# Dealing side work out to TensorE by its time beside a selective scan, taking its results up later, and summing more softmax rows on ScalarE

## The chip, the core and the metric

The kernel runs on one core of a Trainium2 chip, in float32. The metric is the device time in microseconds (us) of one execution, from start to end. Lower is better.

## The reference, cut to what matters

Four layers work on `x` of shape (4, 128, 64, 64), that is four images of 128 channels and 4096 pixels. The change touches the first three.

```
# layer 0: for every image
u  = groupnorm(x)
s  = scores(u)        # depthwise 3x3, gelu, channel attention, depthwise 3x3, gelu, head, variance
order = argsort(-patch_mean(s))            # 256 patches of 4x4 pixels
x1 = layernorm(u[order] + pe[order])
xc = silu(conv1d(x1 @ in_proj));  z = x1 @ in_proj_z
dt = softplus(...);  B, C = xc @ x_proj
h_t = exp(dt_t * A) * h_(t-1) + dt_t * B_t * xc_t     # 256 channels x 16 states, 4096 steps of t
y   = (sum over states of h * C + D * xc) * silu(z)
x   = x + (y @ out_proj)[inverse order]
# layer 1
x   = x + conv3x3(groupnorm(x), 128 -> 128 channels) + bias
# layer 2, attention part: for every image, 16 heads of 8 numbers, 4096 tokens
q   = ring(ln(t)) per head;  e = exp(q q^T / sqrt(8))   # symmetric
ctx = (e @ q) / rowsum(e);   then a projection, norms and a small feed-forward part
# layer 2, second part, and layer 3: expert layers and a linear attention (not touched)
```

## The kernel before

**Layers 0 and 1** are in `layers01`. The image's pixels stand along the free dimension, in eight chunks of 512. Three sections follow each other: the first image is brought into scan order alone (`in_order(0)`), then one long scan section treats all four images, then the last image is finished alone (`end(3)`).

The scan section has 32 chunks (four images of eight), and each chunk has eight steps `g`, one for two of the 16 states. A step does this:

- TensorE spreads two rows of B over the partitions into the PSUM tile `b_ps`, of which there is one buffer.
- VectorE multiplies `dtx` by `b_ps` into `hs` (L637), and then runs four scans of 128 x 512 (L641). Each scan takes its factors from a PSUM tile `decay`, which ScalarE makes with an Exp (L640). There are two such tiles.
- GpSimd copies the carry (L644) and multiplies `hs` by C (L647, two instructions), with C broadcast from DRAM by the DMAs `c_sb<-c_d`.
- TensorE sums over the states into `y_ps`, one step later (`add`).

Between these steps the program places three other kinds of work.

- `enter(n + 1)` makes the inputs of the next chunk: products `xc_ps`, `z_ps`, `dbc_ps`, `dt_ps`, activations Silu (L541, L519), Exp and Ln, three GpSimd products, and DMAs that double the results into `dt2` and `dtx2`. It is a generator whose steps are taken one in a scan step.
- `leave(n)` finishes the chunk before: two VectorE instructions (L592), a GpSimd product with the gate `sz` (L595), the product `out_ps`, and a ScalarE copy (L600).
- `others(b)` is what this text calls the work beside the scan. It is `end(b - 1)`, which puts the image before back into its pixel order and convolves it (`put_back`, then `convolve` with `groupnorm_padded` and `conv3x3`), followed by `in_order(b + 1)`, which prepares the next image.

The work beside is a generator too. It stops at 141 points where both parts exist, at 106 for the first image, and at 35 for the last. The count of stops decides how much is placed in a scan step:

```python
due = BESIDE * (NG * c + g) // (NG * NCH - NG - 1) if c > 0 or g > 1 else 0
```

`BESIDE` is 140, so two or three stops fall on a step, whatever lies between them: a 3x3 convolution of a whole chunk (9 products of 512 columns) counts as one stop, as a tiny group norm product does. A stop's products and the instruction that takes up their result from PSUM stand together in the program. All of these products draw on the same three PSUM buffers (tag `mm`).

In the scan section the order of TensorE's instructions is the order in which the program writes them (`manual_schedule(engines={PE})`). The order on VectorE, ScalarE, GpSimd and the DMA queue is made by a scheduler that starts from the program's order.

Exp and Tanh use one function table of ScalarE; Gelu, Silu, Ln and Sqrt use others, and a change of table is an instruction of its own (ACT_TABLE_LOAD).

**Layer 2's attention** goes image by image, head by head. For a head, 16 pairs of key tiles `m` meet four blocks of 1024 queries `j`. Because `e` is symmetric, only pairs with `m // 4 >= j` are computed. A step (one `j`, one `m`) has four score products, two Exps of 128 x 1024 on ScalarE (L1153), and eight passes of `ctx_ps`. In a step with `m // 4 > j` (the program calls it `behind`) VectorE also transposes both Exps in 32 x 32 blocks into `turned` (L1140, L1159), for later products `acc_ps`, and the row sums of the Exps are needed. The row sums come in one of two ways. Either ScalarE's accumulator delivers them, at one ACTIVATION_READ_ACCUMULATOR after each Exp; or GpSimd folds the step's two Exps twice (L1101, L1102), and VectorE reduces the quarter, five steps later (L1146). The function `folded` chooses. TensorE, VectorE and GpSimd keep the program's order here.

A step of the `behind` kind needs, on VectorE, two transposes. The order of steps inside a block is three, two or one `behind` steps and then one on the diagonal.

Of the kernel before, what the change touches and what calls it, by code (L numbers as in the profile page):

```python
# [9 lines left out]
F32 = mybir.dt.float32  # L10
# [19 lines left out]
class Common:  # L30
# [3 lines left out]
    def __init__(self, tc, pool):  # L34
        nc = self.nc = tc.nc
# [85 lines left out]

    def groupnorm_padded(self, xb, xp, small, psum):
# [4 lines left out]
        for c in range(NCH):  # L127
            nc.vector.bn_stats(st[:, c, :], xb[:, c * CH : (c + 1) * CH])
            if c % 2:
                yield  # L130
        mv = small.tile([P, 2], F32, name="gn_mv")
        nc.vector.bn_aggr(mv, st)
        yield
        mp = psum.tile([P, 1], F32, name="gn_mp", tag="mm")
        self.mm(mp, self.group_mean, mv[:, 0:1])
        gm = small.tile([P, 1], F32, name="gn_gm")
        nc.vector.tensor_copy(gm, mp)
        d = small.tile([P, 1], F32, name="gn_d")
        nc.vector.tensor_tensor(d, mv[:, 0:1], gm, ALU.subtract)
        v2 = small.tile([P, 1], F32, name="gn_v2")  # L140
        nc.vector.scalar_tensor_tensor(v2, d, d, mv[:, 1:2], ALU.mult, ALU.add)
        yield
        vp = psum.tile([P, 1], F32, name="gn_vp", tag="mm")
        self.mm(vp, self.group_mean, v2)
        sd = small.tile([P, 1], F32, name="gn_sd")
        nc.scalar.activation(sd, vp, AF.Sqrt, bias=self.eps5)
        rs = small.tile([P, 1], F32, name="gn_rs")
        nc.vector.reciprocal(rs, sd)
# [3 lines left out]
        nc.gpsimd.memset(xp[:, 1 : HW + 1, HW + 1 : HW + 2], 0.0)  # L152
        off = small.tile([P, 1], F32, name="gn_off")
        nc.vector.scalar_tensor_tensor(off, gm, -1.0, rs, ALU.mult, ALU.mult)
        yield
        for c in range(NCH):
# [7 lines left out]
            if c % 2:  # L164
                yield

    def conv3x3(self, ps, taps, xp, c):

        for k in range(9):
# [4 lines left out]
                xp[:, 8 * c + ky : 8 * c + ky + 8, kx : kx + HW],  # L174
# [43 lines left out]
def layers01(K, xd, dpool, w, w1):  # L218
# [6 lines left out]
    BESIDE = 140  # L225
    with ExitStack() as ctx:
# [81 lines left out]

        deep1 = depthwise(w["conv1_w"], "deep1")
# [6 lines left out]
        def in_order(b, made, work, psum):  # L316
# [39 lines left out]
            yield  # L356
            unders = [under, gather(xp, 1)]
            for c in range(NCH):
                ps = convolved(unders.pop(0), deep1)
                nc.scalar.activation(  # L360
# [8 lines left out]
                yield  # L369
# [4 lines left out]
            yield  # L374
# [3 lines left out]
            nc.scalar.activation(c1, c1p, AF.Relu)  # L378
            yield
# [3 lines left out]
            nc.scalar.activation(ca, c2p, AF.Sigmoid)  # L383
# [4 lines left out]
            for c in range(NCH):  # L388
# [5 lines left out]
                nc.scalar.activation(sq, mp, AF.Square)  # L394
                yield
                ps = convolved(unders.pop(0), deep2)
                f2 = work.tile([P, CH], F32, name="f2", tag="ln_xc")
                nc.scalar.activation(f2, ps, AF.Gelu, bias=conv2_b, scale=ca)
                if c + 2 < NCH:
                    unders.append(gather(fp, c + 2))  # L400
                yield
# [3 lines left out]
                nc.scalar.activation(pv, vp, AF.Tanh, scale=5.0)  # L405
                yield
# [3 lines left out]
                nc.scalar.activation(sc, hp, AF.Tanh, bias=head_b, scale=0.5)  # L410
                yield
# [7 lines left out]
                yield  # L419
# [4 lines left out]
            for h in range(2):  # L424
# [12 lines left out]
                yield  # L437
# [6 lines left out]
            for h in range(2):  # L444
# [10 lines left out]
                yield  # L455
# [4 lines left out]
            for c in range(NCH):  # L460
# [11 lines left out]
                yield from K.layernorm_steps(xl, x1, work, psum)  # L472
                yield
# [8 lines left out]
                yield  # L482
# [5 lines left out]
            for o in range(0, 16, 2):  # L488
# [5 lines left out]
                nc.vector.tensor_copy(ts, tp)  # L494
                yield
# [3 lines left out]
                nc.scalar.copy(by_rank[:, o : o + 2, :], pp)  # L499
                yield  # L500
            made.append((xq, perm_inv))

        def scan(seqs, others, work, psum, psbc, psex, psy):
# [17 lines left out]
            def enter(n):  # L521
# [9 lines left out]
                for d in range(2):  # L531
# [10 lines left out]
                    if n > 0:  # L542
                        gate(n - 1, d)
# [43 lines left out]
            def leave(n):  # L587
# [8 lines left out]
                yield  # L596
                op = psum.tile([P, CH], F32, name="out_ps", tag="mm")
                for d in range(2):
                    mm(op, out_projT[:, d, :], xc[:, d, :], start=d == 0, stop=d == 1)
                nc.scalar.copy(seqs[b][0][:, c * CH : (c + 1) * CH], op)  # L600
# [26 lines left out]
            for n, (b, c) in enumerate(chunks):  # L627
                if c == 0:
                    carry = small.tile([P, NG, NQ], F32, name="carry", bufs=2)
                    nc.vector.memset(carry, 0.0)  # L630
                    beside, done = others(b), 0
# [1076 lines left out]
```

## Time and profile before

| what | us |
|---|---|
| median of three runs | 11060.14 (11053.74 to 11065.5) |
| the profiled execution, its own time | 11065.94 |
| its span in the trace | 11064.2 |
| first image alone, up to the first decay | 273.6 |
| scan section, first decay to last | 2842.9 |
| of it, images 0, 1, 2, 3 | 695.2, 761.6, 760.9, 625.3 |
| the last image's end and the first image's attention inputs | 288.7 |
| the four attention blocks | 1370.4, 1375.6, 1373.6, 1375.4 |
| between them, three times | 270 to 271.3 |
| everything after | 1352.0 |

An image's share of the scan section runs from its first `decay` to the next image's first. An attention block runs from its first score product to its last. In the views of waits a row reads: engine, tile and line of the instruction that was late, then what released it, then the sum, the number and the longest of such waits. In the view of stretches a row gives the stretch, its length, and then for each engine the busy time and the number of instructions, at last the granted TensorE clock, the DMA share and the rate.

### The profile page before, as it was taken

How to read it: one execution, taken by the hardware profiler on the slowest of the kernel's cores; microseconds unless marked ns; L12 is line 12 of the kernel's file. 1: busy time of each engine (PE TensorE's matmuls, PEld its weight loads, DVE VectorE, ACT ScalarE, POOL GpSimd, SP SyncE). 2: the span in 40 equal slices, each digit the busy share in tenths (PEclk: the TensorE clock that was granted, in tenths of full speed). 3: DMA queues.
4: the chain of work that ended last, by engine and by line, in shares of the span. 5: the costliest groups of instructions: out<-in, count | busy, mean ns of one | idle time of the engine just before them, and what ended most of it. 6: DMA issues, size and time to landing. Idle time of an engine off the chain costs nothing. (4 is left out here: it accounts for less than half of the span.)

```text
span 11064.2 us, 183405 instructions
## 1 busy us (share of the span) xinstructions
PE 9097.1 (82%) x71376; PEld 3379.2 (31%) x71376; DVE 7816.5 (71%) x8718; ACT 7349.4 (66%) x9690; POOL 6134.3 (55%) x3623
## 2 busy tenths in 40 slices
PE   5777878778766999968999968999968999966767
PEld 2222223223122333323333323333323333323433
DVE  2688687687846887867788867888757788744563
ACT  2565464654526999857998857989958889932431
POOL 0466455455626777736777736777737777720000
PEclk8787888878778999979999979999979999977888
DMA  3322322322212121222221121212122112122004
GB/s 86 82 71 52 97 60 57 100 63 64 54 48 42 33 37 35 33 72 36 36 36 33 32 77 34 38 32 33 32 77 38 33 33 33 32 87 87 22 16 137
DMA packets 524325, 581.54 MB, mean 53 GB/s; under 512 B 106232, under 2 KB 329536, under 8 KB 520896
## 3 DMA queue, kind: packets, MB, share of 16 engines
q1 hardware_dynamic: 523456, 569.81, 22.2%
q8 instruction: 563, 9.22, 0.4%
q14 instruction: 306, 2.51, 0.1%
HBM read 373.96 MB, written 76.55 MB: 41 GB/s over the span
## 5 line engine op out<-in xcount | busy, mean ns | idle before, releaser
L1153 ACT ACTIVATE ex<-score 128x1024 f32<-128x1024 f32 x5120 | 4904.9, 1031 | 555.5 <-issue 221.2
L1101 POOL TENSOR_TENSOR folded<-ex 128x1024 f32<-128x1024 f32 x960 | 2293.0, 2389 | 1163.5 <-ACT ex L1153 1131.4
L89 PE MATMUL ctx_ps<-ex,qt 128*32 128x512 f32 x20480 | 2723.7, 596 | 0.0
L1159 DVE STREAM_TRANSPOSE turned<-ex 128x1024 f32<-128x1024 f32 x1536 | 1892.0, 1232 | 479.2 <-ACT ex L1153 394.2
L89 PE MATMUL acc_ps<-turned,turned_v 128*32 128x256 f32 x24576 | 1827.5, 389 | 220.2 <-DVE turned L1140 218.8
L1140 DVE STREAM_TRANSPOSE turned<-ex 128x1024 f32<-128x1024 f32 x1536 | 1854.7, 1207 | 0.0
L89 PE MATMUL score<-queries,keys 32*128 32x512 f32 x10240 | 1358.8, 497 | 124.5 <-ACT ex L1153 74.7
L641 DVE TENSOR_TENSOR_SCAN hs<-decay,carry,hs 128x512 f32<-128x512 f32 x1024 | 1248.2, 1263 | 153.4 <-ACT decay L640 144.1
L640 ACT ACTIVATE decay<-dt,a_neg 128x512 f32<-128x512 f32 x1024 | 699.9, 690 | 876.7 <-DVE hs L641 873.1
L1102 POOL TENSOR_TENSOR quarters<-folded 128x512 f32<-128x512 f32 x960 | 1234.5, 1286 | 75.3
L647 POOL TENSOR_TENSOR hs<-hs,c_sb 128x1024 f32<-128x1024 f32 x512 | 1202.2, 2370 | 47.8 <-DMA c_sb<-c_d 28.0
L89 PEld LDWEIGHTS score<-queries,keys 32*128 32x128 f32 x10240 | 523.5, 182 | 2183.5 <-issue 1670.8
L89 PEld LDWEIGHTS acc_ps<-turned,turned_v 128*32 128x32 f32 x24576 | 561.7, 108 | 937.6 <-issue 543.9
L89 PE MATMUL y_ps<-hs,pair 128*64 128x512 f32 x2048 | 657.3, 760 | 225.1 <-POOL hs L647 225.1
L89 PEld LDWEIGHTS ctx_ps<-ex,qt 128*32 128x32 f32 x20480 | 684.7, 110 | 463.3 <-DVE ctx L1083 53.4
L637 DVE TENSOR_TENSOR hs<-dtx,b_ps 128x2048 f32<-128x2048 f32 x256 | 581.6, 2272 | 321.2 <-PE b_ps L89 227.2
L644 POOL COPY carry<-hs 128x4 f32<-128x4 f32 x256 | 65.2, 255 | 1110.3 <-DVE hs L641 1095.8
L1146 DVE TENSOR_REDUCE dacc<-quarters 128x2 f32<-128x512 f32 x960 | 617.4, 648 | 0.0
L1083 DVE COPY ctx<-ctx_ps 128x512 f32<-128x512 f32 x256 | 177.2, 692 | 564.2 <-PE ctx_ps L89 564.1
L89 PE MATMUL ln_var<-ln_sq,mean 128*128 128x512 f32 x448 | 297.1, 750 | 223.6 <-ACT ln_sq L104 188.2
L973 POOL TENSOR_TENSOR turned_v<-v,quarter 128x1024 f32<-128x1024 f32 x192 | 459.0, 2392 | 16.7 <-DMA v<-value_d 11.1
L89 PE MATMUL b_ps<-dbc,spread 32*128 32x512 f32 x512 | 341.7, 751 | 145.8 <-DVE hs L637 145.8
(344 smaller groups left out, 9306.9 us busy)
## 6 DMA issues: line engine op xcount, KB each, us to landing
c_sb<-c_d SPq DMA_DIRECT2D x512, 128.0 KB
queries<-head_d SPq DMA_DIRECT2D x1024, 64.0 KB
keys<-head_d SPq DMA_DIRECT2D x1024, 64.0 KB
dt<-dt SPq DMA_DIRECT2D x128, 256.0 KB
dtx<-dtx SPq DMA_DIRECT2D x128, 256.0 KB
w<-in_L_ffn_weight SPq DMA_DIRECT2D x32, 1024.0 KB
w<-in_L_ffn_weight SPq DMA_DIRECT2D x128, 256.0 KB
under<-xp SPq DMA_DIRECT2D x384, 66.0 KB
```

Source lines behind the costliest of these rows:

```text
L89: self.nc.tensor.matmul(out, lhsT, rhs, start=start, stop=stop)
L637: nc.vector.tensor_tensor(hs, dtx2, bb.unsqueeze(1).to_broadcast([P, NQ, CH]), ALU.mult)
L640: nc.scalar.activation(ex, dt2[:, q, :], AF.Exp, scale=a_neg[:, q, g : g + 1])
L641: nc.vector.tensor_tensor_scan(hs[:, q, :], ex, hs[:, q, :], carry[:, g, q : q + 1], ALU.mult, ALU.add)
L647: nc.gpsimd.tensor_tensor(at, at, cs.unsqueeze(1).to_broadcast([P, 2, CH]), ALU.mult)
L973: nc.gpsimd.tensor_tensor(t, v.unsqueeze(2).to_broadcast([P, 4 * BT, 4, HD]), quarter.unsqueeze(1).to_broadcast([P, 4 * BT, 4, HD]), ALU.mult,
L1101: nc.gpsimd.tensor_tensor(hs, exs[:, :, 0], exs[:, :, 1], ALU.add)
L1102: nc.gpsimd.tensor_tensor(qs, hs[:, :, 0 : CH // 2], hs[:, :, CH // 2 :], ALU.add)
L1140: nc.vector.transpose(*upright)
L1146: nc.vector.tensor_reduce(at, qs, AX.X, ALU.add)
L1153: nc.scalar.activation(ex, sps[p], AF.Exp, scale=scale, accum_out=dacc[:, j, h, t : t + 1] if summed else None)
L1159: nc.vector.transpose(*upright)
```

## The change

The change has six parts.

1. The stops of the work beside the scan carry a cost each, in units near a microsecond of TensorE, and the scan deals out by sums of costs (`COST_END` 127.2 for `end`, `COST_ORDER` 215.2 for `in_order`). The total is that of the parts which the image has, so the first and the last image's work is spread over seven chunks as well. Inside a chunk the table `ROOM` gives 4% of the chunk's share up to the second step, 21% up to the fourth, and then 20% to each of the last four.
2. Instructions that take up a product's result are not written with it, but put on a list (`K.late`), which is emptied (`flush`) at fixed places of a scan step, ahead of the next piece of work beside.
3. The entry of a chunk begins at step 0, not 1, and has one step more: the second half of `xc_ps` and both `z_ps` come a step after the first half. In `leave` the product `out_ps` comes one step later.
4. The 3x3 convolution works in pieces of 256 columns, of which there are 16, not 8.
5. The layer norm of `in_order` copies the centred values out of PSUM on ScalarE and multiplies them on GpSimd. Before, VectorE did both in one instruction.
6. In the attention, a third of the `behind` steps of block 0 is folded, where it was two thirds. A fold's reduction may come three steps later, and only in a step on the diagonal, or where more than five folds are waiting.

The diff, cut to its core:

```diff
+    def flush(self):
+
+        for f in self.late:
+            f()
+        self.late.clear()
...
     def conv3x3(self, ps, taps, xp, c):
...
-                xp[:, 8 * c + ky : 8 * c + ky + 8, kx : kx + HW],
+                xp[:, 4 * c + ky : 4 * c + ky + 4, kx : kx + HW],
...
-    BESIDE = 140
+
+    COST_END, COST_ORDER = 127.2, 215.2
+    ROOM = (0.04, 0.04, 0.09, 0.21, 0.41, 0.61, 0.81, 1.0)
...
+        later = lambda f, *args, **kw: K.late.append(lambda: f(*args, **kw))
...
                 ps = convolved(unders.pop(0), deep1)
-                nc.scalar.activation(
+                later(
+                    nc.scalar.activation,
...
-                yield
+                yield 5
...
-                yield from K.layernorm_steps(xl, x1, work, psum)
-                yield
+                mp = psum.tile([P, CH], F32, name="pos_xc", tag="mm")
+                mm(mp, K.center, x1)
+                sq = work.tile([P, CH], F32, name="ln_sq")
+                later(nc.scalar.activation, sq, mp, AF.Square)
+                later(nc.scalar.copy, xl, mp)
+                yield 1.2
...
+                    nc.gpsimd.tensor_tensor(xl, xl, rs.rearrange("p a b -> p (a b)"), ALU.mult)
...
                     nc.scalar.activation(xc[:, d, :], ps, AF.Silu, bias=conv1d_b[:, d : d + 1])
-                    if n > 0:
+                    if d == 0:
+                        yield
+                if n > 0:
+                    for d in range(2):
                         gate(n - 1, d)
...
                 nc.gpsimd.tensor_tensor(xc, xc, sz, ALU.mult)
                 yield
+                yield
                 op = psum.tile([P, CH], F32, name="out_ps", tag="mm")
...
-                    beside, done = others(b), 0
+                    beside, done = others(b), 0.0
+                    total = (COST_END if b > 0 else 0) + (COST_ORDER if b + 1 < NB else 0)
...
-                    due = BESIDE * (NG * c + g) // (NG * NCH - NG - 1) if c > 0 or g > 1 else 0
+                    K.flush()
+
+
+                    share = (c + ROOM[g]) / (NCH - 1)
+                    due = (total * share if share < 1 else math.inf) if c > 0 or g > 2 else 0
                     if done < due:
-                        next(beside, None)
-                        done += 1
+                        done += next(beside, due)
                     if g + 1 < NG or n + 1 < len(chunks):
                         m = NG * n + g + 1
                         bb, cs = spread_b(*divmod(m, NG)), spread_c(*divmod(m, NG))
+                    K.flush()
                     if g > 0:
                         next(leaving, None)
-                        next(coming, None)
+                    next(coming, None)
                     while done < due:
-                        next(beside, None)
-                        done += 1
+                        K.flush()
+                        done += next(beside, due)
...
-            for c in range(NCH):
-                ps = psum.tile([P, CH], F32, name="conv", tag="mm")
+            for c in range(2 * NCH):
+                ps = psum.tile([P, CH // 2], F32, name="conv", tag="mm")
                 K.conv3x3(ps, taps, xp, c)
-                at = xb[:, c * CH : (c + 1) * CH]
-                nc.vector.scalar_tensor_tensor(at, ps, bias, at, ALU.add, ALU.add)
-                yield
+                at = xb[:, c * CH // 2 : (c + 1) * CH // 2]
+                later(nc.vector.scalar_tensor_tensor, at, ps, bias, at, ALU.add, ALU.add)
+                yield 4.5
...
-                return ((m - 4) % 3 < 2, m % 2 == 0, m % 4 < 3)[j]
+                return ((m - 4) % 3 == 0, m % 2 == 0, m % 4 < 3)[j]
...
-                folds.append((n + 5, qs, at))
+                folds.append((n + 3, qs, at))
...
-                while folds and folds[0][0] <= n:
+
+                while folds and (folds[0][0] <= n and not behind or len(folds) > 5):
```

The other stops get costs in the same way: 1 to 4 in the group norm, 4 or 5 for a gathered convolution, 1.2 for single products, 3.4 for a pair of permuted columns. The other products' results go on the list in the same way.

## The prediction

> **What bounds the kernel now.** I read the profile in this order: the busy shares, the busy time by stretch with one stretch a scan chunk or an attention block, the waits of the engine that carries the scan, and last a timeline of one attention head. The whole span first:
>
> ```profile
> span 11064.2 us, 183405 instructions
> PE 9097.1 (82%) x71376; PEld 3379.2 (31%) x71376; DVE 7816.5 (71%) x8718; ACT 7349.4 (66%) x9690; POOL 6134.3 (55%) x3623
> ```
>
> No engine is full on average, so the stages have to be read. These stretches are four scan chunks of image 1, one of image 3 with nothing beside it, and the first attention block:
>
> ```profile
> 968.80:1052.30 83.50, 67.63 (x216) 29.89 (x216) 67.53 (x61) 41.47 (x59) 51.94 (x34) 0.88 0.24 59
> 1052.30:1168.40 116.10, 103.13 (x243) 39.58 (x242) 71.14 (x67) 42.04 (x59) 48.07 (x28) 0.91 0.15 39
> 1168.40:1289.20 120.80, 89.40 (x333) 29.64 (x333) 68.43 (x62) 60.99 (x85) 53.07 (x39) 0.84 0.42 116
> 1473.50:1570.00 96.50, 67.28 (x140) 19.06 (x140) 83.40 (x81) 57.07 (x79) 54.85 (x34) 0.78 0.22 60
> 2979.30:3050.90 71.60, 51.41 (x113) 14.04 (x112) 60.21 (x45) 37.28 (x51) 49.37 (x29) 0.71 0.23 60
> 3405.20:4775.60 1370.40, 1299.84 (x14548) 463.59 (x14551) 1100.78 (x1166) 1229.95 (x1567) 1047.56 (x558) 1.00 0.20 32
> ```
>
> A bare scan chunk takes 71.6 us, 8.95 a step, and VectorE is busy for 60.2 of them. The chain of scans on VectorE is the bound, and 11.4 us of it stand still. With work beside it a chunk takes up to 120.8 us, though VectorE's work grows by 7 to 23 us only. Against 71.6 a chunk the four images lose 123, 189, 188 and 53 us, 553 together. What VectorE waits for in image 1 says where that goes:
>
> ```profile
> DVE hs L637 <- PE b_ps L89: 78.1, 20, 18.9
> DVE xb L703 <- PE conv L89: 37.9, 8, 9.0
> DVE hs L641 <- ACT decay L640: 24.5, 17, 4.0
> DVE ln_vt L109 <- PE ln_var L89: 11.3, 4, 6.7
> ```
>
> The reader is to see that `b_ps`, a product of about a microsecond, comes up to 18.9 us late: it stands in TensorE's fixed order behind the pieces of work beside. And VectorE, which works in order, stands eight times at a convolution that was not finished (37.9 us).
>
> An attention block is another matter: TensorE is busy for 1299.8 of 1370.4 us at full clock. Its idle time before `acc_ps` and ScalarE's pace are in these rows (the first from the waits of all four blocks, the others from the timeline of one head):
>
> ```profile
> PE acc_ps L89 <- DVE turned L1140: 218.8, 312, 1.6
> ...
> 4007.87 0.19 ACT L1153 ACTIVATION_READ_ACCUMULATOR ex<-score 128x1 f32 x1
> ...
> 4009.24 6.57 ACT L1153 ACTIVATE ex<-score 128x1024 f32<-128x1024 f32 x7 [0.18 <-PE score L89]
> ```
>
> **The change, part by part: the dealing by cost.** A convolution block of 9 products took 64.06/8 = 8.0 us where TensorE ran dense after the scan. In image 1 the program before puts 2, 2, 3 and 1 blocks into four following steps: 16, 16, 24 and 8 us. A bare chunk's own TensorE work is 51.4 x 0.71 / 8 = 4.6 us a step at full clock, so a step of 8.95 has room for 4.3. The four steps overrun by 11.7 + 11.7 + 19.7 + 3.7 = 47 us; the chunk lost 44.5. In the changed program's order the same work lies as 8, 12, 8, 8 and 4 us and then 4 to 8 in five more steps: overruns of 3.7 + 7.7 + 3.7 + 3.7 + 3.7 = 22. The first depthwise pieces (12 gathered products, 281.0/1536 x 24 = 4.4 us) go from 2, 2, 3, 1 a step (18 us over) to 1, 2, 2, 2, 1 (14). The steps ahead of the convolution and the later parts lose by this sum: 3 + 14 us over before, 7 + 27 after. Image 1 then overruns by some 70 us where it was 82; the first image by 12 for 25; the last, which had all its blocks in the first two chunks, by nothing for 49.
>
> **Results a step later.** The remaining loss of image 1, 189 - 82 = 107 us, is waiting inside a step: product, activation, next product. VectorE's floor is its work: it did 552 us in image 1 against 481 in eight bare chunks, so 71 of the 189 are work that stays. The most that images 0 to 3 can give is 78, 118, 118 and 40, 354 together. I take 60, 85, 85 and 40, 270 us: images 1 and 2 keep 104 each, the overrun of 70 and half of the VectorE work that the overrun does not cover, and the rest goes. The bounds are 86 (the overruns' differences, 13 + 12 + 12 + 49, alone) and 354.
>
> **What that costs.** ScalarE's table changes go from 506 to 591 in the program's order, nearly all in the scan section; a bare chunk has 8 for 6, because both gates now stand alone. The row is 1283 ns, so 85 x 1.283 = 109 us of ScalarE, which is busy for 1525 of 2843 us there. They matter only where two `decay` tiles are used up before the table is back; the row `hs <- decay` above is 24.5 us in an image with 85 changes, so 0.29 us for each, and I take 25 us (0 to 109). The Trainium skill, ScalarE: Activation LUTs, section What ACT_TABLE_LOAD costs, speaks against the change: it [...]counts 1283 ns and a drain of about 1380 ns for every change. The trace has the 1283, but no drain: in a bare chunk a `decay` Exp, the load and the Ln follow each other within 0.05 us. By the rule it would be 226 us of ScalarE time and some 50 on the path. I keep the trace's.
>
> **Entry, gates, `leave`.** `out_ps` waited for GpSimd's gate product in 25 places, 95.0 us of TensorE in the scan section; a step later it is there. The cover is the step's other products. This is inside the 270. Entry from step 0 moves eight passes (some 3.5 us) and the DMA `c_d` forward; `dt2` and `dtx2` (eight DMAs a chunk, 0.74 to 0.80 us of issue each) are not issued earlier than the chunk's later steps. VectorE waited 29.5 us for `dtx` in the scan section, so 0 to 29 of gain: none taken. On SP's queue the 576 gathers of 0.59 us stay, 7.1 us for one piece. Up to 72 follow each other before and up to 36 after. `c_sb` stands behind them, and GpSimd waited for it only 28 us in all; taken as nothing, 15 either way.
>
> **Smaller pieces.** The Trainium skill, Perfetto Trace Analysis, section Matmuls, holds larger matmuls to be more efficient. In this trace passes of 256 columns (`perm_p`) start 0.22 us apart at full clock and passes of 512 (`conv`) 0.43, so 576 passes of 0.43 become 1152 of 0.22: 248 and 253 us, five more. If the rule were felt as a weight load in the open (0.19), it would be up to 109. I take 3. VectorE pays 64 x 0.39 for 32 x 0.75 (1 us). The norm's copy is 32 x 0.585 on ScalarE and about 32 x 1.19 on GpSimd (by the row of L465), for 32 x 0.67 off VectorE: all beside the scan, and within 5 us in the first section of 273.6, where ScalarE has gaps of a microsecond in each norm.
>
> **The attention.** 256 folds go: GpSimd loses 256 x (2.39 + 1.29), VectorE 256 x 0.648 = 166 us, ScalarE gains 512 x 0.208 = 106 us. Query block 0 of a head takes 35.9 us between its score products. VectorE needs there 12 x 2.44 for transposes, 8 x 0.648, 3 x 0.41 and 0.69: 36.4, so it is the bound; after, 33.8. TensorE without its waits needs about 33.9, ScalarE 16 x 2 x 0.938 + 16 x 0.208 = 33.3 after. The gaps before `acc_ps`, about 2 us a head here, can close. But a summed step costs ScalarE 2.29 and TensorE passes some of them in 1.43 to 1.87, and three score tiles hold one step and a half. In the order of this block ScalarE falls behind at 8, 12, 14 and 15, by 1.5 us a head after TensorE's slack. The reductions moved to diagonal steps help blocks 1 and 2 by some 0.3. I take 0.8 us a head, 64 heads: 50 us (30 lost to 130 won).
>
> **Sum.** Against the profiled execution: 11065.9 - 270 + 25 + 3 - 50 = 10774. The median is 5.8 below that execution, so about 10768; I say 10768.
>
> **The rivals.** *Full hiding:* 354 in the scan, 130 in the attention, nothing paid: 10576, say 10600. For it: VectorE's own work is then the only floor; against it: overruns that remain in images 1 and 2. *Little:* only the overruns differ, since TensorE's work is the same and `b_ps` keeps its place behind a piece in the order: 86 off, attention nothing: 10974. For it: 11.4 us idle in a chunk with nothing beside. *Slower: ScalarE becomes the bound.* If all added table changes and accumulator reads lie on the path, 109 + 106 = 215 us, and the scan gives only 86, it is 11060 + 129 = 11189. It decides from where what is put on the path exceeds what the dealing gives; the place would be `hs <- decay` in the scan and `score <- ex` in the attention. Against it: ScalarE has 54% in the scan section, and 90% in the attention. *Nothing:* the scheduler undoes the later places; the orders of ScalarE and VectorE do differ, so this is small.
>
> **How the numbers follow.** My forecast has 0.60, full hiding 0.15, little 0.17, slower 0.05, nothing 0.03. A measurement of this kernel can tell about 0.2%, 22 us, from no change. Faster takes the first three but for 0.01: 0.91; same 0.04; slower 0.05. The range leaves out the outer half of full hiding and the slower case: 10610 to 10975.
>
> **What would show it.** Right: the three `b_ps`, `xb` and `ln_vt` rows above fall to under a third; image 3's chunks 0 and 1 come to about 75 us, image 1's eight chunks near 676 in all, with none over 105; 591 table loads; attention blocks of about 1360 with fewer waits of `acc_ps` for `turned` and 416 accumulator reads for 288. Wrong: a scan section over 2750 us, `hs <- decay` far over 144.1 us (what it is in the section now), or blocks over 1376.

## The result, and the profile after

The changed kernel takes 10963.0 us (median of 4, 10954.3 to 10978.5) beside 11058.1 for the kernel before (4 runs). The ratio is 0.9915, with a 95% interval of 0.9898 to 0.9932. It is faster by 95 us, where 290 were forecast; the time lies in the range, but far from the number. The page's first lines:

```profile
span 10952.5 us, 184078 instructions
PE 9041.6 (83%) x71952; PEld 3464.4 (32%) x71952; DVE 7656.5 (70%) x8462; ACT 7514.8 (69%) x10319; POOL 5233.6 (48%) x3143
```

VectorE lost 160 us of work and GpSimd 901, ScalarE gained 165. On VectorE and GpSimd that is the folds, as forecast; on ScalarE it is the accumulator reads (239.1 us before, 346.9 after) and the 85 added table loads of 1.283 us. The span is 111.7 us shorter in the profiled executions. From the two traces, cut at the first `decay` of every image and at the first and last score product:

| stretch, us | before | after | forecast of the difference |
|---|---|---|---|
| scan, image 0 | 695.2 | 674.9 | -60 |
| scan, image 1 | 761.6 | 771.0 | -85 |
| scan, image 2 | 760.9 | 768.0 | -85 |
| scan, image 3 | 625.3 | 571.6 | -40 |
| four attention blocks | 5495.3 | 5449.6 | -50 |
| everything else | 2726 | 2717 | 0 |

Attention and image 3 came as forecast or better. Images 1 and 2, which were to bring 170 us, lost 16. The forecast's +25 for table loads and +3 for pieces are to be read with the images. Busy time by stretch shows where in image 1 it went: its chunks 0 to 3, 5 and 6, then chunk 4 of image 3, then the first attention block (columns: window, its length, PE, PEld, DVE, ACT, POOL busy, granted clock, DMA share, GB/s):

```profile
951.20:1042.20 91.00, 67.36 (x212) 31.32 (x210) 73.53 (x73) 44.43 (x60) 51.87 (x34) 0.86 0.23 57
1042.20:1121.50 79.30, 73.79 (x261) 39.42 (x260) 64.28 (x55) 48.37 (x64) 48.54 (x28) 0.97 0.22 54
1121.50:1205.80 84.30, 71.98 (x248) 38.46 (x246) 66.71 (x54) 39.88 (x53) 49.64 (x32) 0.93 0.25 70
1205.80:1322.80 117.00, 79.82 (x294) 24.16 (x294) 68.15 (x59) 66.41 (x87) 53.29 (x35) 0.80 0.35 96
1409.80:1500.10 90.30, 70.58 (x240) 20.78 (x236) 69.34 (x59) 62.58 (x81) 49.40 (x28) 0.89 0.37 92
1500.10:1640.60 140.50, 94.37 (x210) 35.94 (x210) 86.77 (x90) 82.70 (x111) 67.71 (x45) 0.69 0.16 44
2795.50:2864.50 69.00, 60.77 (x186) 25.71 (x184) 61.23 (x49) 39.92 (x52) 48.46 (x29) 0.90 0.24 61
3345.80:4703.00 1357.20, 1297.99 (x14544) 464.04 (x14544) 1061.58 (x1102) 1239.51 (x1695) 813.32 (x430) 1.00 0.20 33
```

The two convolution chunks, 116.1 and 120.8 us before, are at 79.3 and 84.3: 73 us won. In image 3, whose chunk 4 now carries four half pieces, one a step, the chunk takes 69.0 us, less than the 71.6 of a chunk without any work beside it in the kernel before. But chunk 6, 88.9 before, is at 140.5, chunk 3 went from 96.9 to 117.0, chunk 0 from 83.5 to 91.0 and chunk 7 from 71.5 to 81.6: 89 us lost. Chunks 4 and 5 give back 7. The sum is +9. The dealing did what was forecast for the work that is long on TensorE, and took it back where other work was pressed together.

VectorE's waits in image 1 say what it stands for (us in total, times, longest):

```profile
DVE hs L687 <- ACT decay L686: 57.3, 32, 7.6
DVE hs L683 <- PE b_ps L90: 56.5, 26, 7.8
DVE hs L683 <- DMA dtx<-dtx: 17.3, 1, 17.3
DVE xb L328 <- PE conv L90: 16.3, 5, 5.4
DVE gn_st L135 <- DMA xb<-in_x: 14.3, 1, 14.3
DVE perm_s L328 <- PE perm_t L533: 13.8, 3, 4.7
DVE ln_vt L505 <- PE pos_var L90: 10.1, 5, 2.8
```

`b_ps` and the convolution fell together by 43 us, and the longest wait for `b_ps` from 18.9 to 7.8. But `decay` rose from 24.5 to 57.3, and two long single waits for DMAs are there, one for the image's load and one for `dtx2`.

### The profile page after: what moved, and what is told of

Same layout as the page of the kernel before. It is cut to its first block, busy times and chain, and to the rows that moved or that the text cites. A ratio compares the mean times of both kernels' runs of the same rounds, so it can differ in the third digit from the quotient of the medians.

```text
span 10952.5 us, 184078 instructions
## 1 busy us (share of the span) xinstructions
PE 9041.6 (83%) x71952; PEld 3464.4 (32%) x71952; DVE 7656.5 (70%) x8462; ACT 7514.8 (69%) x10319; POOL 5233.6 (48%) x3143
## 5 line engine op out<-in xcount | busy, mean ns | idle before, releaser
L1151 POOL TENSOR_TENSOR folded<-ex 128x1024 f32<-128x1024 f32 x704 | 1679.4, 2386 | 2073.6 <-ACT ex L1204 2062.0
L687 DVE TENSOR_TENSOR_SCAN hs<-decay,carry,hs 128x512 f32<-128x512 f32 x1024 | 1253.0, 1266 | 200.3 <-ACT decay L686 186.0
L1152 POOL TENSOR_TENSOR quarters<-folded 128x512 f32<-128x512 f32 x704 | 905.1, 1286 | 55.2
L1197 DVE TENSOR_REDUCE dacc<-quarters 128x2 f32<-128x512 f32 x704 | 453.4, 644 | 8.0 <-POOL quarters L1152 8.0
L90 PE MATMUL ln_var<-ln_sq,mean 128*128 128x512 f32 x384 | 240.2, 710 | 182.9 <-ACT ln_sq L105 158.1
L90 PE MATMUL b_ps<-dbc,spread 32*128 32x512 f32 x512 | 319.4, 706 | 70.7 <-DVE hs L683 70.7
```

The costliest lines, as they stand in the source:

```text
L90: self.nc.tensor.matmul(out, lhsT, rhs, start=start, stop=stop)
L687: nc.vector.tensor_tensor_scan(hs[:, q, :], ex, hs[:, q, :], carry[:, g, q : q + 1], ALU.mult, ALU.add)
L1151: nc.gpsimd.tensor_tensor(hs, exs[:, :, 0], exs[:, :, 1], ALU.add)
L1152: nc.gpsimd.tensor_tensor(qs, hs[:, :, 0 : CH // 2], hs[:, :, CH // 2 :], ALU.add)
L1197: nc.vector.tensor_reduce(at, qs, AX.X, ALU.add)
```

## The experiments

The theories, by the names that the expectations use. T1: the costs are TensorE's time, so a layer norm, whose TensorE part is short and whose ScalarE, VectorE and GpSimd parts are long, is dealt out two or three to a step. T2: the norm's new form, with its copy on ScalarE and its multiplication on GpSimd, is what costs. T3: the group norm behind the image's load has costs of 8 for a wait of some 30 us. T4: the added table loads and the late results cost more than was counted. Each run has its own comparison with the kernel before (11046 to 11053 us); ratios are to that.

**The attention part alone**, in the kernel before:

```diff
-return ((m - 4) % 3 < 2, m % 2 == 0, m % 4 < 3)[j]
+return ((m - 4) % 3 == 0, m % 2 == 0, m % 4 < 3)[j]
-folds.append((n + 5, qs, at))
+folds.append((n + 3, qs, at))
-while folds and folds[0][0] <= n:
+while folds and (folds[0][0] <= n and not behind or len(folds) > 5):
```

> The kernel before with the attention's part of the change alone (one diagonal step in three folded, the reductions on diagonal steps). Theory: the four attention blocks give what they gave in the changed kernel, 45.6 us in all, and the scan section stays at 2843: about 11013, ratio 0.996. Rival (the attention's gain comes only with the late results ahead of it): within 10 us of before.

11003.8 us, ratio 0.9954 (0.9939 to 0.9969). The four blocks take 5449.2 us, 46 less, and the scan section 2842.8. The attention's gain is of its own, and the scan's is the rest. The scan program is the same in this kernel and in the one before, and their traces differ by up to 4 us in an image (621.6 for 625.3 in image 3): differences of that size between images say nothing.

**Norms costed by more than TensorE** (chunk 6):

```diff
-    later(nc.scalar.copy, xl, mp);  yield 1.2
+    later(nc.scalar.copy, xl, mp);  yield 5
-    K.late.append(normed);          yield 1.2
+    K.late.append(normed);          yield 4
-    ... xn ...                      yield 0.5
+    ... xn ...                      yield 1
-COST_END, COST_ORDER = 127.2, 215.2
+COST_END, COST_ORDER = 127.2, 272.0
```

> The changed kernel with the three stops of a norm costed 5, 4 and 1 instead of 1.2, 1.2 and 0.5 (sum for the arrangement raised by 56.8), so that one norm, not two or three, falls into a step. Theory T1 (norms are short on TensorE but cost ScalarE some 5.5 us each, so three in a step stop decay and the scans): chunk 6 of images 1 and 2 falls from 140 to about 100 us, the eight convolution-side chunks pay 5 to 10 us for being dealt denser, total 60 us under the changed kernel, about 10900. T2 (the norm's form is what costs): chunk 5 and chunk 6 together lose the same as now, total within 15 us of 10963.

10921.9 us, ratio 0.9880 (0.9866 to 0.9895). Busy time by stretch, chunks 0, 2 and 6 of image 1:

```profile
945.80:1047.10 101.30, 76.29 (x227) 36.35 (x226) 79.65 (x77) 52.81 (x72) 51.90 (x34) 0.82 0.21 51
1133.60:1231.80 98.20, 64.32 (x205) 30.39 (x207) 72.92 (x65) 48.12 (x63) 50.25 (x36) 0.81 0.32 92
1522.90:1617.50 94.60, 65.03 (x168) 24.83 (x168) 68.42 (x62) 63.02 (x85) 57.05 (x36) 0.77 0.19 51
```

Chunk 6 fell from 140.5 to 94.6, as T1 has it. But chunks 0 and 2 rose by 10 and 14, because the rest is dealt out faster when more of the image's budget belongs to the norms. Image 1 won 12 us of the 46. What happens inside a crowded step can be seen in ScalarE's timeline in step 4 of chunk 6, a step of 26 us with three norms, in the changed kernel (start, us, then the idle time before in brackets):

```profile
1572.73 1.28 ACT L507 ACT_TABLE_LOAD   x1
1574.02 0.32 ACT L507 ACTIVATE ln_sd<-ln_vt,eps 128x16 f32<-128x16 f32 x1
1574.25 0.57 ACT L328 COPY xl<-pos_xc 128x512 f32<-128x512 f32 x1
1574.83 1.28 ACT L686 ACT_TABLE_LOAD   x1
1576.13 0.69 ACT L686 ACTIVATE decay<-dt,a_neg 128x512 f32<-128x512 f32 x1
1580.10 1.42 ACT L516 ACTIVATE xn<-xl,norm_b,norm_g 128x256 f32<-128x256 f32 x2 [3.28 <-POOL xl L511]
1581.33 0.68 ACT L686 ACTIVATE decay<-dt,a_neg 128x512 f32<-128x512 f32 x1
```

and VectorE's two scans there:

```profile
1576.85 1.28 DVE L687 TENSOR_TENSOR_SCAN hs<-decay,carry,hs 128x512 f32<-128x512 f32 x1 [1.41 <-ACT decay L686]
1582.04 1.28 DVE L687 TENSOR_TENSOR_SCAN hs<-decay,carry,hs 128x512 f32<-128x512 f32 x1 [3.90 <-ACT decay L686]
```

On ScalarE the `xn` of a norm waits 3.28 us for GpSimd's multiplication, the next `decay` starts only behind it, and the scan waits 3.90 us for that. None of it is TensorE's time.

**The norm's form:**

```diff
-later(nc.scalar.copy, xl, mp)
+later(nc.vector.tensor_copy, xl, mp)
-nc.gpsimd.tensor_tensor(xl, xl, rs, ALU.mult)
+nc.vector.tensor_tensor(xl, xl, rs, ALU.mult)
```

> The changed kernel with the norm's copy and its multiplication on VectorE instead of ScalarE and GpSimd; same stops, same costs. T2 (the form, with ScalarE's copy and GpSimd's multiplication, is what makes chunk 6 long): chunk 6 of images 1 and 2 falls from 140 to about 110, total 50 us under the changed kernel. T1 (too many norms in one step, whoever copies): chunk 6 stays over 130, and total is within 20 us of 10963, rather above it, since VectorE takes 24 x 1.3 us more.

10919.1 us, ratio 0.9879 (0.9862 to 0.9895): 44 us under the changed kernel, near T2's 50. But chunk 6 falls to 129.5 only, where T2 had 110 and T1 more than 130, so crowding (T1) is the larger part of that chunk, and neither theory holds whole. The form has 11 us in chunk 6, and 8 each in image 0 and in the first section. VectorE did 13 us more in chunk 6 and the chunk was still shorter; `decay` is waited for 42.6 us in image 1, where it was 57.3. **Both edits together:**

> The changed kernel with a norm costed 5, 4, 1 (as in the run that came to 10922) and its copy and multiplication on VectorE (as in the run that came to 10919). If the two have different causes (norms crowded in a step; ScalarE and GpSimd crowded by the norm's form), they add up: total about 10880. If they are the same cause: about 10915.

10907.7 us, ratio 0.9869 (0.9854 to 0.9884). Between the two expectations, nearer to the second: they share most of their cause. Images 1 and 2 are at 748.5 and 747.5.

**Room for the image's load** (chunk 3):

```diff
+xb = image(b)
+yield 20
-yield from K.groupnorm_padded(image(b), xp, small, psum)
+yield from K.groupnorm_padded(xb, xp, small, psum)
-COST_END, COST_ORDER = 127.2, 215.2
+COST_END, COST_ORDER = 127.2, 235.2
```

> The changed kernel with a stop of cost 20 between the issue of the image's load and the group norm's first statistics (sum for the arrangement raised by 20). T3 (TensorE stands 27.5 us at gn_mp because the statistics wait for the load, and b_ps stands behind it): the wait of gn_mp for gn_mv in chunk 2/3 falls from 27.5 us to a few, chunk 3 of images 1 and 2 falls from 117 to about 95, and total is some 40 us under the changed kernel, about 10925. Rival (chunk 3 is long by its 96 depthwise products of 4.4 us a dozen, not by the load): chunk 3 stays over 110 and total within 10 us.

10988.5 us, ratio 0.9943 (0.9928 to 0.9958): slower, where T3 had a gain. The row `gn_st <- xb` fell from 14.3 to 5.3 us, the longest wait of `gn_mp` from 27.5 to 17.7 only, and chunk 3 from 117.0 to 110.2, but chunks 0, 4 and 7 of image 1 rose by 7, 6 and 5, and image 0, which has no store to wait for, by 26. A pause that is paid for out of the same steps makes all the others denser. **Stores and loads in quarters** make the load earlier and cost no step:

```diff
-nc.sync.dma_start(out=t, in_=x[b])
+for i in range(4): nc.sync.dma_start(out=t[:, quarter(i)], in_=x[b][:, quarter(i)])
-nc.sync.dma_start(out=xd[b], in_=xb)
+if c % 4 == 3: later(nc.sync.dma_start, out=xd[b][:, quarter(c // 4)], in_=xb[:, quarter(c // 4)])
```

> The changed kernel with the convolution's result stored in four quarters as they are finished and each image loaded in four quarters, so that the load behind the store starts sooner. Theory (step 7 of chunk 2 takes 32.3 us, since VectorE stands 14.3 us at the first statistics and TensorE 27.5 at gn_mp for the load): the wait of gn_st falls under 7 us, chunk 2/3 loses 10 us in each of images 1 and 2, total about 20 us under the changed kernel, 10943. Rival (the load's issue stands behind c_sb in SP's queue, whatever its size): gn_st's wait stays over 12 us and total is within 8 us.

10946.7 us, ratio 0.9901 (0.9885 to 0.9918). VectorE's row in chunk 3 of image 1:

```profile
DVE gn_st L135 <- DMA xb<-in_x: 3.8, 3, 3.2
```

14.3 became 3.8, chunk 3 fell to 107.9, images 1 and 2 by 11 and 7. So T3 is right about the wait, at about 10 us an image. Over the whole, the interval overlaps that of the changed kernel.

**The transfers `dt2` and `dtx2` on another queue:**

```diff
-nc.sync.dma_start(out=t[64 * z : 64 * z + 64]..., in_=src[64 * a : 64 * a + 64])
+nc.gpsimd.dma_start(out=t[64 * z : 64 * z + 64]..., in_=src[64 * a : 64 * a + 64])
```

> The changed kernel with the eight transfers dt2 and dtx2 of a chunk issued on GpSimd's queue, so that they do not stand behind the gathers of the depthwise convolution in SP's queue. Theory (step 7 of chunk 3 takes 24.5 us because dtx2 comes 17.3 us late behind up to 26 gathers of 0.6 us): that wait goes, chunk 3 of images 1 and 2 falls by 15 us each, total 20 to 40 us under the changed kernel, about 10930. Rival (dtx is late because dt and the decay before it are late): the wait stays and total is 0 to 40 us above, since GpSimd pays for issuing 256 transfers.

11028.8 us, ratio 0.9977 (0.9968 to 0.9986), worse than the rival had. In image 1 the wait for `dtx` fell from 17.3 to 5.1 us and chunk 3 to 105.7, as the theory has it: in SP's queue these transfers stood behind the gathers. But the wait moved and did not go. Over the whole scan section it was 67.6 us, five times, in the changed kernel; now VectorE's row reads:

```profile
DVE hs L683 <- DMA dtx<-dtx: 84.1, 13, 19.1
```

Image 3, which had no such wait, has 28.8 us of it, and waits 39.0 us for the convolution where it was 13.8; it went from 571.6 to 624.4. GpSimd is busy for 61.0 us in chunk 0 of image 1 where it was 51.9, and that chunk takes 104.5 us.

**One part undone alone.** The entry as before (each gate behind its half of the convolution, `leave` with one stop less), which brings back 58 table loads:

```diff
-if g > 0: next(leaving, None)
-next(coming, None)
+if g > 0: next(leaving, None); next(coming, None)
```

> The changed kernel with the entry as before: each gate stands directly behind its half of the entry convolution, entry begins at step 1, leave has one stop less. ScalarE then has 533 table loads instead of 591. T4 (what the changed kernel loses in images 1 and 2 is the price of the added loads: decay waits of 57 us in image 1 where it was 24.5): the decay wait falls by half, total 40 us under the changed kernel, about 10920. Rival (the later out_ps and gates are part of the gain, as the prediction counted them): bare chunks go from 69.5 back to 71.6, and total is 40 to 80 us above the changed kernel, about 11020.

10998.3 us, ratio 0.9954 (0.9937 to 0.9970). T4's gain is out: with 58 loads fewer, the scan section is 37 us longer, 23 of it in image 3. The edit moves the loads and the entry together, so it does not price the loads alone; the kernels with other functions, below, do. The rival's mechanism is in TensorE's waits in the scan section of this run:

```profile
PE out_ps L90 <- POOL xc L636: 134.7, 31, 8.6
```

In the changed kernel the section has no such row. And `decay`, with fewer loads, is waited for longer: 219.6 us for 186.0 in the section.

**Results taken up at once** (`later` runs its instruction in place, and so do `variance`, `scale` and `normed`):

> The changed kernel with every result taken up in its own stop instead of behind the next flush (part 2 undone alone). By the prediction's second step (waiting inside a step is what the late results remove, some 107 us in image 1) it gives back most of the scan's gain: total over 11020. If the results' place hardly matters, because the scheduler or the length of a step separates product and result anyway: within 20 us of 10963.

10995.6 us, ratio 0.9949 (0.9934 to 0.9964). The scan section is 31 us longer: 16, 7, 3 and 4 in images 0 to 3. The late results help, but in images 1 and 2 they are worth 7 and 3 us, hardly more than two traces of one program differ by, and not the tens that the forecast gave them.

**Whole convolution pieces** of 512 columns, cost 9:

> The changed kernel with whole convolution pieces of 512 columns, cost 9 (part 4 undone alone). If the smaller pieces matter for b_ps (a step's overrun is rounded up to a piece of 8 us instead of 4): chunks 1 and 2 of images 1 to 3 lengthen by 5 to 10 us each, total 30 to 50 us above the changed kernel. If only the cost matters: within 15 us of 10963.

10948.2 us, ratio 0.9907 (0.9892 to 0.9922); the interval overlaps the changed kernel's. Image 3 is 15 us longer, images 1 and 2 shorter by 4 and 10. The smaller pieces pay where the convolution is alone beside the scan, and nothing over the whole. Chunks 4 to 6 of image 3, with two whole pieces each, take 74.9, 76.0 and 74.5 us, where four half pieces took 69.0, 69.7 and 69.5: 5 to 6 us, where the prediction's overrun of 3.7 a piece gives 7.4.

**Dealing by count.** A first form began in step 2 of chunk 0, and there put back the image before while its last chunk's output was still to be written:

```diff
-share = (c + ROOM[g]) / (NCH - 1)
-due = (total * share if share < 1 else math.inf) if c > 0 or g > 2 else 0
+due = 154 * (NG * c + g) // (NG * NCH - NG - 1) if c > 0 or g > 1 else 0
```

> The changed kernel with the work dealt out by the number of stops, evenly over the steps and at the pace of before (154 stops due in every image), in place of their cost (part 1 undone alone; late results, entry and smaller pieces stay). If the dealing by cost is what brought image 3 from 625 to 572 and image 0 from 695 to 675, both come back to within 15 us of before, total about 11020. For images 1 and 2 the prediction has it 60 us worse than the changed kernel (overruns); T1 (dealing by TensorE's time alone gathers the norms and takes back what it gives to the convolution) has it equal within 15 us, with chunk 6 near 90 and chunk 1 near 110.

11109.0 us, ratio 1.0053 (1.0038 to 1.0068). With `g > 2`:

> The changed kernel dealt out by the number of stops (154 due in every image, evenly over the steps, from step 3 of chunk 0 on), everything else as changed. An even deal that began one step earlier had a scan section of 2934 us, images 712, 800, 802 and 620. Expected: the same within 15 us, total about 11105, which is 50 us slower than the kernel before: late results, entry and pieces alone lose, and the costs bring some 145 us. Rival: the one step was what made it long, and the section comes to 2850 or less.

11102.2 us, ratio 1.0043 (1.0028 to 1.0058), scan section 2934.1: slower than before, as expected. Within the changed program the costs are worth 148 us of the section. Images 1 and 2, at 799.8 and 805.5, are as in the first form, some 30 us above the changed kernel, which is neither the 60 nor the equality that was expected of that form: chunk 1 is at 92.6, but chunk 3 at 136.9. The parts of the change do not add up; the new stops without the costs lose.

**What is left in images 1 and 2.** With the mends above together:

> The changed kernel with the three mends together: norm costed 5, 4, 1; its copy and multiplication on VectorE; results and images moved in quarters. Apart they gave 41, 44 (the first two 55 together) and 16 us under the changed kernel. If they add up: about 10892. If the quarters give nothing once the norms are spread: about 10908.

10908.6 us, ratio 0.9871 (0.9855 to 0.9888): the quarters give nothing once the norms are spread. Is ScalarE's table the rest? Three kernels with another function in the place of Gelu, Tanh, Sigmoid and Sqrt:

```diff
-AF.Gelu, AF.Tanh, AF.Sigmoid, AF.Sqrt
+AF.Relu, AF.Identity, AF.Identity, AF.Identity
```

> The changed kernel with another function in the place of every Gelu, Tanh, Sigmoid and Sqrt of the arrangement, group norm and layer norms (Relu or Identity of the same shape), which leaves ScalarE 273 table loads for 591; only the scan section is read. Theory (what still separates images 1 and 2 from the forecast 676 is ScalarE: each piece beside brings two table loads, in a queue in which decay waits): images 1 and 2 fall from 771 to 700 or less. Rival (waits of products, load and gathers, whatever the table): over 745.

> The kernel before with the same functions replaced (195 table loads for 506); only the scan section is read. If the table loads were as dear before the change as after it, images 1 and 2 fall from 761 by as much as in the changed kernel; if they got dear by the dealing (crowded norms), by less than half of that.

> The kernel with the three mends, with the same functions replaced; only the scan section is read. If the crowding of the norms was the only thing that the loads made dear, images 1 and 2 stay near 740; if every piece pays for its loads, they fall below 690.

| image 1 | with its tables | without | loads in the image |
|---|---|---|---|
| before | 761.6 | 747.3 | 85, 42 |
| changed | 771.0 | 756.6 | 109, 64 |
| three mends | 745.1 | 730.2 | 112, 64 |

Each of these three was read from one execution. Some 15 us each in image 1, 0.3 us for a load taken away, before and after alike; in image 2 it is 10 us before, and 17 in both others. The theory's 700 is far off: the loads are not the rest. In the changed kernel chunk 6 stays long without its loads:

```profile
1473.00:1599.10 126.10, 90.29 (x210) 33.25 (x210) 85.75 (x90) 65.50 (x98) 67.85 (x45) 0.73 0.18 49
```

So most of the crowding there is not the loads. That it is the chain from engine to engine is what the timeline above suggests, and no run shows it alone. Is it TensorE's own time? One tap of nine, four products of twelve:

```diff
-for k in range(9):
+for k in range(1):
-for kx in range(3):
+for kx in range(1):
```

> The changed kernel with one of the nine products of a convolution piece and four of the twelve of a depthwise piece (the other taps are left out), everything else in place; only the scan section is read. If TensorE's time beside the scans is the price that remains (a step has no 4.3 us of free room), chunks 1 to 5 of image 1 fall from 79, 84, 117, 87, 90 to within 5 us of a bare 69.6 but for VectorE's own work, 60 us in all over the image. If the price is waiting (loads, gathers, results, VectorE's work), they fall by less than 25 us in all.

Image 1 takes 737.0 (one execution). The convolution's chunks 1 and 2 are all but free now:

```profile
1030.20:1102.80 72.60, 61.62 (x136) 18.16 (x134) 63.95 (x57) 48.41 (x63) 49.40 (x28) 0.74 0.22 55
1102.80:1175.10 72.30, 47.52 (x117) 14.29 (x116) 64.64 (x53) 39.89 (x52) 49.34 (x32) 0.78 0.22 70
```

They lost 19 us, and chunks 3 to 5 lost 17 of the 86 that they have over three times 69.4, which is what chunks 4 to 6 of image 3 take in the changed kernel. So TensorE's time is most of what the convolution costs, and most of what the depthwise stage costs is something else. The five chunks gave 35 us, between the two expectations. The cut has a side effect: in the same run chunks 4 to 6 of image 3 came to 75.7, 72.6 and 74.4 us, longer with a ninth of their convolution, at a granted clock of 0.78 where it was 0.89 to 0.92. Why is open, so 35 us is what the missing products gave net.

**The permutation costed twofold**, on top of the norms' costs and form:

```diff
-later(nc.vector.tensor_copy, ts, tp);                yield 1.2
+later(nc.vector.tensor_copy, ts, tp);                yield 2.4
-later(nc.scalar.copy, by_rank[:, o : o + 2, :], pp); yield 2.2
+later(nc.scalar.copy, by_rank[:, o : o + 2, :], pp); yield 4.4
-COST_END, COST_ORDER = 127.2, 272.0
+COST_END, COST_ORDER = 127.2, 299.2
```

> The kernel with norms costed 5, 4, 1 and their copy and multiplication on VectorE, and with the pieces of the permutation costed 2.4 and 4.4 instead of 1.2 and 2.2, so that two pieces fall into a step and not four. If crowded permutation pieces (the steps of up to 27 us at the end of chunk 6) are like the crowded norms, chunk 6 and step 0 of chunk 7 lose 15 us an image, of which the denser deal takes back 5: about 10880. Rival (what one stage is given is taken from another): within 12 us of 10908.

10892.9 us, ratio 0.9866 (0.9849 to 0.9882). This is the fastest, and its interval lies clear of the changed kernel's; against the kernel without this last edit it does not. Chunks 1, 2 and 6 of image 1:

```profile
1037.00:1127.90 90.90, 85.88 (x319) 51.63 (x319) 64.88 (x54) 39.79 (x54) 47.58 (x27) 0.97 0.19 47
1127.90:1235.40 107.50, 76.74 (x259) 31.55 (x257) 70.28 (x64) 55.78 (x73) 55.11 (x39) 0.83 0.33 95
1528.80:1606.60 77.80, 66.66 (x204) 28.52 (x204) 69.86 (x62) 54.03 (x70) 49.03 (x28) 0.87 0.21 54
```

Chunk 6 came down from 140.5 to 77.8, but chunks 1 and 2 are at 90.9 and 107.5, and the image at 744. The time moved from one stage to another. Four ways of spreading the norms have image 1 between 744 and 759 us.

## Why the prediction was right or wrong

- **What bounds the kernel.** Right: the chain of scans on VectorE, with TensorE's order in front of `b_ps`. The convolution's chunks show it: with most of TensorE's taps gone they take 72.6 and 72.3 us, no more than chunks 4 to 6 of image 3 in the same run. In the crowded chunks it is not the whole: there `decay`, on ScalarE, is waited for longer than `b_ps` (19.4 us for 5.5 in chunk 6 of image 1).
- **The dealing by cost, for the convolution and image 3.** Right, and low for image 3: -54 for -40. Some 23 of the 54 go with the later entry, since image 3 takes 594.6 us without it. Chunks 0 and 1 came to 79.1 and 74.4 where 75 was expected.
- **Images 1 and 2, 85 us each: the step that failed.** Of each 85, 12 were the difference of TensorE's overruns, and 73 were to come out of the 107 us of waiting inside a step, which "results a step later" was to remove. That is the term that failed: undoing the late results alone costs 7 and 3 us. (VectorE's 552 us in image 1 read 555.6 in the trace, so its work that stays is 74, not 71.) The overrun sum was also wrong in what it counted. It read 70 for 82, so a gain of 12; the convolution alone won 73, and crowded stages whose TensorE time is small lost 89. Costs of TensorE are blind to a norm, to a load and to a gather. By runs, in image 1: spreading the norms takes 46 us off chunk 6 and 12 off the image; the load 11 off the image; the late `dtx` 11 off chunk 3, and nothing off the image.
- **The norm's form, nothing in the scan and within 5 us in the first section.** Wrong, and a second failed term: it was put at nothing from each engine's busy time alone. With its copy and multiplication back on VectorE the kernel is 44 us faster; in the traces 8 us of it are in the first section, and 8, 13 and 7 in images 0 to 2. Work was taken off the engine that bounds the scan and put into the queues of ScalarE and GpSimd; in the timeline above `decay` starts behind it.
- **Image 0, -60.** -20: the same crowding, its chunks 5 and 6 at 100.7 and 94.7 (72.7 and 71.5 before).
- **VectorE's rows.** `b_ps`, `xb` and `ln_vt` were to fall under a third in image 1. They went from 78.1, 37.9 and 11.3 to 56.5, 16.3 and 10.1. `decay` in the whole section rose from 144.1 to 186.0, which the text named as a sign of being wrong, as it did a section over 2750 us (it is 2785.6).
- **Table loads, +25.** 591, as counted, and the size fits: 0.3 us for each load taken out of image 1, times 85, is 27. That rate is of other loads; no run takes the added ones away alone. The Trainium skill, ScalarE: Activation LUTs, section What ACT_TABLE_LOAD costs, has a drain of some 1380 ns at every switch. In the timeline above the load that starts at 1574.83 follows the end of the copy within 0.01 us, and the `decay` behind it starts at 1576.13, 0.02 us after the load's end, so no drain is seen here.
- **Entry, gates, `leave`, in the 270.** Right in kind: without it `out_ps` waits 134.7 us, and the section is 37 us longer. It shared in the gain although it added 58 of the 85 loads.
- **SP's queue, taken as nothing, 15 either way.** Wrong in its victim. The text looked at `c_sb` behind the gathers; the one that came late was `dtx2`, 67.6 us in the section where it was 29.5. GpSimd's queue was no way out: 84.1.
- **Smaller pieces, +3.** Not told from nothing.
- **Attention, -50.** -46, by itself, and in the place that was named: query block 0. Accumulator reads are 416 a block, and TensorE's wait of `acc_ps` for `turned` fell from 218.8:

```profile
PE acc_ps L90 <- DVE turned L1190: 177.4, 311, 2.1
L1204 ACT ACTIVATION_READ_ACCUMULATOR ex<-score 128x1 f32 x416 | 86.7, 208 | 0.0
```

  The working behind the number does not fit, so its closeness is in part luck. It has query block 0 of a head at 35.9 us and VectorE, with 36.4, as its bound. These are block 0 of one head before and after, from its first score product to that of block 1 (columns as above):

```profile
4010.50:4044.30 33.80, 31.83 (x350) 10.94 (x347) 28.91 (x32) 30.71 (x39) 27.51 (x15) 1.00 0.05 11
4027.70:4060.90 33.20, 31.85 (x352) 10.98 (x348) 25.84 (x28) 31.19 (x45) 13.38 (x7) 1.00 0.05 12
```

  Before it took 33.8 us, as in most heads, and TensorE was the busiest in it, with 31.8 us to VectorE's 28.9. The change won 0.6 us a head there. Fewer folds and later reductions were not run apart.
- **The rivals.** *Little* gave 10974 by another way, and was nearest: it had 86 from the scan and nothing from attention; the runs have 57 and 46. *Slower*, ScalarE as the bound in the scan, holds for single steps only.

Open: an even deal leaves some 745 us in images 1 and 2, 190 over eight chunks of 69.4. By single runs 15 of it go with the table loads and, in the changed kernel, 35 with TensorE's taps. VectorE does 71 us (the changed kernel) to 86 us (the last one) more in image 1 than in eight chunks of 60.2; that this work stays on the path was not shown by a run. How the rest divides was not settled.

## What to carry to other kernels

When work is dealt out beside a bound chain, cost each piece by the queue in which the chain's own next instruction stands behind it, not by one engine: a piece that is short on TensorE can hold up ScalarE's order, VectorE's first statistics or the DMA queue. Sum such a forecast stage by stage for every stage whose density changes, since a stage that gets room takes it from another. Work taken off the bound engine is not won if it goes into a queue in which the chain's next instruction stands: here 44 us came back by giving the norm's copy and multiplication to VectorE again. And test the parts one by one: here the new entry, late results and pieces without the costs were slower than the kernel before.

## What the hardware showed that was not expected

Four half pieces of convolution beside a chunk, one a step, seem to cost nothing: the chunk takes 69.0 us, and with one product of nine left in each piece it was not shorter (75.7). Issuing 256 transfers from GpSimd's queue instead of SP's did not end the late transfers but moved them (84.1 us of waits for 67.6), and image 3 took 624.4 us for 571.6. Taking away 45 table loads from an image of 109 was worth 14 us, a quarter of their 58 us of ScalarE time, and 17 in the next image.
